# An attention and mixture-of-experts block: all tokens through sorted slots of 256 places, with places, splits and norm roots on GpSimd

## The chip, the cores and the metric

The kernel runs on one core of one Trainium2 chip. The metric is the device time of one execution in microseconds (us). The engines are called PE (TensorE: matmuls and transposes), DVE (VectorE), ACT (ScalarE), POOL (GpSimd) and SP (SyncE, which here only issues DMAs). Each engine works through its own queue in order: an instruction that waits holds up all that stand behind it on the same engine.

## The reference

x has 2 batches of 1024 tokens of 128 numbers, in f32. LN is a layer norm without weights.

```
x = x + LN(attention(LN(x)))     # 8 heads, 2 groups of keys, latent of 32, causal softmax
x = x + LN(moe(LN(x)))

scores = sigmoid(h @ gate.T)                  # 32 experts in 4 groups of 8
keep the 2 groups whose two best (score + bias) add up highest
of their experts keep the 6 with the highest score + bias
w = scores of these 6, divided by their sum, times 0.2
out = sum of w_e * down_e(silu(gate_e h) * up_e h)        # expert width 64
    + shared expert (width 64)
    + 0.1 * the one anchor expert (of 16, width 32) that the best expert points to
```

A token needs the weights of 2 of the 4 groups alone. A group holds 8 experts and 4 anchors: 640 columns, 5 chunks of 128.

## The kernel before, in words

**Schedule.** The order of the instructions on every engine is written out by hand. The main program emits the work of attention and then of the experts. All else is written as Python generators in three lists, `ends`, `moves` and `side`. `tick()` (L251) advances one waking generator in each list by one piece; a `yield n` lets it sleep for n ticks. So each piece's place in the engines' queues is set by the tick at which it is emitted.

**Attention.** There are 16 units (batch, group of keys, block of 256 tokens) and 40 steps in the loop of `attention()` (L590). A step makes the scores `s` (L519) with a bias matmul that subtracts the maxima (L533), the exp on ACT (L539), a mask on POOL on the diagonal (affine_select, L542), the values `o` (L556) and the sums (L565). The maxima come from an earlier pass over the scores (`sm`, L454, L464, reduced on DVE to `nm`, L471). `nm` is split into three bf16 parts on DVE (L487, L489: three casts, two subtractions per unit), which PE transposes (`pm`, L498) into `mT`.

**Routing.** The tokens are four parts of 512. `route` (L669) is a generator per part: output projection `po` (L685), layer norm, sum with x, second layer norm, router logits `pl`, and the choice of groups and experts on DVE. A layer norm's root is `Norm.root` (L335, with its lines L338 and L339): Ln and Exp on ACT, then Newton's step on DVE (L341).

**Sorting.** Three parts are sparse. `place_first` (L971) sorts the first two together, `place_second` (L998) the third: rank matmuls on PE, then operations on DVE give each token two places, and rows of 176 numbers (the token and its weights) are moved to DRAM `placed` by indirect DMAs on POOL (L921), 16 and then 8, each behind a memset (L920), one per tick. Places are in slots of 256, and a slot belongs to one group. `numbered` (L931) makes the slots' group numbers on DVE; `numbers_of` (L949) loads them into registers on PE and SP, and so puts a wait for that DVE work into both queues.

**Slots.** `Slots` (L1035) runs 15 slots. Each fetches its group's weights `wbs` (640 KB, L1025) and its rows `got` (L1062), turns the rows on PE (`pt_s`), writes the weights of the experts to DRAM and reads them back as `spreads`, spread over partitions (L1089, L1094). It makes `pgs` and `pus` on PE (`hidden`, L1111), silu on ACT (L1118), two products on DVE (L1119, L1120), the down projection `ys` on PE (L1134) and writes its 256 results with one DMA from ACT's queue (L1141).

**Dense part.** The fourth part goes through all four groups: `experts` (L1231), 20 chunks of 512 tokens (L1264, L1265, L1278). Beside it, the results of the three sparse parts are gathered by 24 indirect DMAs on POOL (`gather`, at L1203), and `finish` and `normed` add the shared expert, normalize and write out (L1210, L1184).

## Time and profile before

| what | us |
|---|---|
| three runs | 506.69, 508.99, 509.77 |
| median of them | 508.99 |
| the profiled execution | 511.09 |
| its span | 509.4 |
| attention, to its last sums matmul | 0 to 274.2 |
| first matmul of slot 0 | 277.5 |
| slots 0 to 14, to the first matmul of the dense part | 277.5 to 419.2 |
| dense part, to the end of its last matmul | 419.2 to 497.1 |
| tail, to the end of the span | 497.1 to 509.4 |
| PE busy, DVE busy | 429.5, 298.4 |
| ACT busy, POOL busy | 221.9, 84.6 |

The span is the time between the first and the last event on the profile's clock; the profiled execution's own time is 1.7 us longer. In a row of the timeline stand the start, the duration, the engine, the line of the kernel, the operation, out<-in with partitions x elements, how many instructions were put together, and in brackets the idle time before with what ended it. In a row of the groups, the numbers behind the first bar are busy time in us and the mean of one instruction in ns; behind the second bar stands the idle time before such instructions. The granted clock is TensorE's, as a share of full speed.

### The profile page before, as it was taken

What the parts mean: (1) busy time and instruction counts of PE and PEld (TensorE: products, weight loads), DVE (VectorE), ACT (ScalarE), POOL (GpSimd) and SP (SyncE); (2) the same over time, 40 slices, a digit from 0 to 9 for tenths busy, and PEclk for the clock granted to TensorE, in tenths of its full rate; (3) what the DMA queues carried; (4) which work ended last, traced back from release to release, by engine and by line L of the source; (5) the groups of instructions that cost most, each with busy time, mean ns of one, the idle gap of its engine ahead of it and who ended that gap; (6) DMA issues with size and microseconds to landing.
All of it is one profiled execution on the core that took longest, in us unless ns stands there. A gap on an engine that the chain in (4) does not pass through costs nothing.

```text
span 509.4 us, 10160 instructions
## 1 busy us (share of the span) xinstructions
PE 429.5 (84%) x3727; PEld 267.1 (52%) x3727; DVE 298.4 (59%) x1046; ACT 221.9 (44%) x464; POOL 84.6 (17%) x160
## 2 busy tenths in 40 slices
PE   8998979999899999959576479599989989945990
PEld 5554544545445555424234368488888974413430
DVE  4479563786967986986204554343775435415882
ACT  3445654566436766326436126345423322122442
POOL 3000000111001201004821005100000005750100
PEclk9999998999989999989759778799999999977996
DMA  7891000000000000001120825666687694614130
GB/s 204 181 280 44 2 1 2 1 2 3 2 1 3 2 1 1 2 22 53 66 72 16 226 80 153 170 208 200 181 240 226 178 266 113 180 44 134 53 93 21
DMA packets 42946, 47.45 MB, mean 93 GB/s; under 512 B 17392, under 2 KB 35936, under 8 KB 42896
## 3 DMA queue, kind: packets, MB, share of 16 engines
q1 hardware_dynamic: 37520, 39.81, 28.3%
q0 software_dynamic: 1920, 3.74, 2.5%
q10 hardware_dynamic: 3456, 3.25, 2.0%
q8 instruction: 30, 0.49, 0.4%
q14 instruction: 20, 0.16, 0.1%
HBM read 38.06 MB, written 11.34 MB: 97 GB/s over the span
## 4 chain that ended last, share of the span: by engine, by line
PE 46%; DVE 26%; DMA 9%; issue 8%; ACT 4%; POOL 4%; SPq 1%; ACTq 0%; POOLq 0%; DVEq 0%
DVE nm L471 9%; PE sm L454 5%; PE s L519 4%; DMA wbs<-wgu 4%; PE o L556 4%; PE pgs L1111 4%; PE ys L1134 4%; PE pus L1111 3%; POOL placed L921 3%; PE pp L407 3%; PE o L565 3%; PE pg L1264 2%; DMA spreads<-cw_slot 2%; PE pu L1265 2%; PE po L685 2%
## 5 line engine op out<-in xcount | busy, mean ns | idle before, releaser
L471 DVE TENSOR_REDUCE nm<-sm 128x1 f32<-128x512 f32 (+2 forms) x192 | 92.7, 548 | 47.6 <-PE sm L464 24.9
L539 ACT ACTIVATE pr<-s 128x512 f32<-128x512 f32 (+1 forms) x160 | 75.6, 558 | 80.5 <-PE s L533 72.2
L519 PE MATMUL s<-qT,kT 32*128 32x256 f32 (+1 forms) x640 | 54.1, 397 | 10.7 <-DVE pos L901 6.3
L1119 DVE TENSOR_TENSOR hids<-hids,pus 128x512 f32<-128x512 f32 x30 | 20.6, 687 | 51.0 <-PE pus L1111 39.9
L519 PEld LDWEIGHTS s<-qT,kT 32*128 32x128 f32 x640 | 35.3, 190 | 28.6 <-issue 16.2
L556 PE MATMUL o<-pr,v 128*32 128x256 f32 (+1 forms) x640 | 43.3, 387 | 7.3 <-issue 5.5
L542 POOL TENSOR_SCALAR_AFFINE_SELECT pr<-pr 128x1024 f32<-128x1024 f32 x16 | 18.1, 1128 | 187.0 <-ACT pr L539 187.0
L454 PE MATMUL sm<-kT,qT 32*128 32x512 f32 (+3 forms) x384 | 45.8, 533 | 1.5 <-DVE nm L471 1.2
L1134 PEld LDWEIGHTS ys<-wd_sb,hids 128*128 128x128 f32 x300 | 42.3, 201 | 5.9 <-DVE hids L1120 1.8
L1134 PE MATMUL ys<-wd_sb,hids 128*128 x300 | 42.9, 285 | 2.2 <-DVE hids L1120 1.4
L1203 POOL DMA_INDIRECT y<-results,place_of x24 | 23.9, 997 | 110.3 <-PE pg L1264 103.3
L565 PE MATMUL o<-pr,ones 128*32 128x256 f32 (+1 forms) x640 | 40.3, 370 | 1.0 <-issue 1.0
L1111 PE MATMUL pgs<-hTp,wbs 128*128 128x256 f32 x120 | 34.6, 414 | 7.4 <-DMA wbs<-wgu 5.1
L1118 ACT ACTIVATE hids<-pgs 128x512 f32<-128x512 f32 x30 | 17.9, 598 | 35.1 <-PE pgs L1111 33.1
L556 PEld LDWEIGHTS o<-pr,v 128*32 128x32 f32 x640 | 17.6, 113 | 29.2 <-issue 19.0
L1111 PE MATMUL pus<-hTp,wbs 128*128 128x256 f32 x120 | 32.9, 399 | 0.0
L1268 ACT ACTIVATE hid<-pg 128x512 f32<-128x512 f32 x20 | 11.8, 597 | 46.8 <-PE pg L1264 26.5
L921 POOL DMA_INDIRECT placed<-rows,place_of x24 | 23.7, 987 | 50.7 <-DVE place_of L911 46.6
L1269 DVE TENSOR_TENSOR hid<-hid,pu 128x512 f32<-128x512 f32 x20 | 13.6, 682 | 29.8 <-ACT hid L1268 9.7
L1278 PE MATMUL oacc<-hid,wd_sb 128*128 128x512 f32 x40 | 21.8, 627 | 9.9 <-DVE hid L1270 9.9
L1120 DVE TENSOR_TENSOR hids<-hids,spreads 128x512 f32<-128x512 f32 (+1 forms) x45 | 27.1, 603 | 3.6 <-DMA spreads<-cw_slot 2.1
L565 PEld LDWEIGHTS o<-pr,ones 128*32 128x32 f32 x640 | 17.5, 110 | 21.8 <-issue 12.6
(270 smaller groups left out, 643.4 us busy)
## 6 DMA issues: line engine op xcount, KB each, us to landing
wbs<-wgu SPq DMA_DIRECT2D x15, 640.0 KB
spreads<-cw_slot SPq DMA_DIRECT2D x30, 256.0 KB
spreadd<-cw_rows SPq DMA_DIRECT2D x16, 256.0 KB
placed<-zero SPq DMA_DIRECT2D x1, 2640.0 KB
got<-placed SPq DMA_DIRECT2D x15, 176.0 KB
wbd<-wgu SPq DMA_DIRECT2D x4, 640.0 KB
spreads<-cw_slot SPq DMA_DIRECT2D x60, 32.0 KB
results<-ys ACTq DMA_DIRECT2D x15, 128.0 KB
```

The costliest lines, as they stand in the source:

```text
L454: nc.tensor.matmul(banks[r][:, at : at + k1 - k0], lhsT=qT[ts(r, L), g, ts(qt, P)], rhs=kT[ts(r, L), g, k0:k1], start=(at == 0), stop=Fals ...
L471: nc.vector.tensor_reduce(nm[:, k0 // BC, j, r : r + 1], banks[r][:, at : at + k1 - k0], AX.X, ALU.max, negate=True,)
L519: nc.tensor.matmul(banks[r][:, at : at + n], lhsT=kT[rows, g, ts(kt, P)], rhs=qT[rows, g, q * QC + lo : q * QC + lo + n], start=(i == 0), ...
L539: nc.scalar.activation(pr[:, r, 0:m], banks[r][:, 0:m], AF.Exp)
L556: nc.tensor.matmul(o[ts(r, L), lo : lo + n], lhsT=qkv[b][2][:, kt, ts(g, L)], rhs=pr[:, r, at : at + n], start=(kt == 0), stop=False, skip ...
L565: nc.tensor.matmul(o[ts(r, L), QC + lo : QC + lo + n], lhsT=ones32, rhs=pr[:, r, at : at + n], start=False, stop=True, skip_group_check=True,)
L921: move = nc.gpsimd.indirect_dma_start(out=placed[:, :], out_offset=bass.IndirectOffsetOnAxis(ap=place_of[:, k, i : i + 1], axis=0), in_=ro ...
L1111: nc.tensor.matmul(p[:, lo : lo + SL], lhsT=wb[:, m, ts(c, P)], rhs=hT, start=(lo == 0), stop=(c == pair[-1]), skip_group_check=True,)
L1120: nc.vector.tensor_tensor(hid[:, 0:n], hid[:, 0:n], sp[:, pair[0] : pair[-1] + 1, :].rearrange("p c t -> p (c t)"), ALU.mult,)
L1134: nc.tensor.matmul(o[:, ts(j, D)], lhsT=hid[:, at : at + P], rhs=w, start=(c == 0 and j == 0), stop=(c == NC - 1), skip_group_check=True,)
L1203: nc.gpsimd.indirect_dma_start(out=y[k][:, t, :], out_offset=None, in_=results[:, :], in_offset=bass.IndirectOffsetOnAxis(ap=place_of[:, k ...
L1278: nc.tensor.matmul(oacc, lhsT=wd_sb[:, c, :], rhs=hid, start=False, stop=(c == NG * NC - 1))
```

## The change

All four parts go through slots. There are 19 of them, and the dense part, its fetches and the gathers are gone.

- **Places.** Each part is placed by itself, in four sets that continue each other: `place(s)` carries the number of slots used, the last open slot of each group (`base`) and how full it is (`taken`). After the rank matmuls and a copy on ACT, 36 dependent operations on POOL give the places. Each part moves its rows by eight indirect DMAs, with two ticks between them.
- **Order of the slots.** `ordered(s)` runs after parts 1, 2 and 3. It sorts the slots so that full ones come first, with 31, 41 and 4 operations on DVE on one partition, and loads the group numbers into registers of PE, SP and POOL and the slots' numbers into SP's. Slots 5 and on wait for the second order and part 2's moves to be emitted, slots 9 and on for the third and part 3's.
- **Results.** The rows carry four more numbers (ROW is 180): where the token's result in each group belongs. A slot reads its row numbers out with a copy on POOL (`to_row`) and scatters its results by token with two indirect DMAs on POOL, instead of one DMA from ACT's queue. `finish(s)` makes the shared expert of its part between the slots. When slot 14 is emitted (the last part: when all are), it reads both results of 512 tokens with one DMA of 512 KB, adds them (POOL for parts 0 to 2, DVE for the last) and normalizes.
- **Splits.** The five operations on `nm` per unit move from DVE to POOL.
- **Roots.** `Norm.root` is eight operations on POOL with `pow`; Ln and Exp on ACT, the Newton operations on DVE and the table loads for them are gone.
- **Sigmoid.** A part that is routed during attention makes it from Exp on ACT and two operations on DVE.
- **Ticks.** From step 8 of attention two side pieces are advanced per tick.

By engine, the instructions go from 204 to 713 on POOL, 1147 to 954 on DVE, 619 to 585 on ACT, 2679 to 2782 on PE and 381 to 424 on SP. On PE, the first load of group numbers stands in step 32 of attention, behind part 1's rank matmuls in step 30; the second at the end of step 39, ahead of the last values and sums and of slot 0, behind part 2's rank matmuls in step 36; the third in slot 5, behind part 3's rank matmuls in slot 4. Slot 0 and 1's rows are turned in step 37. On POOL, the first `to_row` copy stands ahead of part 2's placing, and the roots and sums of `finish(0)` to `finish(2)` stand ahead of the scatters of slots 16 to 18.

The diff, cut to its core:

```diff
-    sparse, dense = [(0, 0, TB), (0, TB, TB), (1, 0, TB)], [(1, TB, TB)]
-    NTS = sum(n for _, _, n in sparse)
+    parts = [(b, t, TB) for b in range(B) for t in range(0, NT, TB)]
+    NTS = TB * len(parts)
     NS = TOPG * NTS * P // SL + NG - 1
+    full_after = [-(-(TOPG * n * TB * P - NG * (SL - 1)) // SL) for n in (2, 3)]
+    ROW = D + E + A + NG
...
         def root(self):
-            tables(EXP_LN)
-            nc.scalar.activation(self.r0, self.var, AF.Ln, bias=eps_t)
-            nc.scalar.activation(self.r0, self.r0, AF.Exp, scale=-0.5)
-        def newton(self):
-            t, r0 = self.t, self.r0
-            nc.vector.tensor_tensor(t, r0, r0, ALU.mult)
-            nc.vector.scalar_tensor_tensor(t, self.var, EPS, t, ALU.add, ALU.mult)
-            nc.vector.tensor_scalar(t, t, -0.5, 1.5, ALU.mult, ALU.add)
-            nc.vector.tensor_tensor(self.rs, r0, t, ALU.mult)
+            eng, v, t, r0 = nc.gpsimd, self.v, self.t, self.r0
+            eng.tensor_scalar(v, self.var, EPS, None, ALU.add)
+            eng.tensor_tensor(r0, v, minus_half.to_broadcast([P, self.n]), ALU.pow)
+            eng.tensor_tensor(t, r0, r0, ALU.mult)
+            eng.tensor_tensor(t, t, v, ALU.mult)
+            eng.tensor_scalar(t, t, -0.5, 1.5, ALU.mult, ALU.add)
+            eng.tensor_tensor(self.rs, r0, t, ALU.mult)
+            eng.tensor_tensor(t, self.mv[:, :, 0], self.rs, ALU.mult)
+            eng.tensor_scalar(self.nb, t, -1.0, None, ALU.mult)
...
         for k in range(3):
             part = parts[:, :, :, k]
-            nc.vector.tensor_copy(part, m0)
+            nc.gpsimd.tensor_copy(part, m0)
             if k < 2:
-                nc.vector.tensor_tensor(m0, m0, part, ALU.subtract)
+                nc.gpsimd.tensor_tensor(m0, m0, part, ALU.subtract)
...
+        eng = nc.gpsimd
+        eng.tensor_scalar(free, taken, -1.0, float(SL), ALU.mult, ALU.add)
+        eng.tensor_tensor(rest, total, free, ALU.subtract)
+        eng.tensor_scalar(more, rest, 0.0, None, ALU.is_gt)
+        eng.tensor_scalar(new, rest, float(SL), None, ALU.is_gt)
+        eng.tensor_tensor(new, new, more, ALU.add)
...
+        eng.tensor_tensor(pos, rank, wide[0], ALU.subtract)
+        eng.tensor_scalar(pos, pos, 0.0, None, ALU.is_ge)
+        eng.tensor_tensor(pos, pos, wide[1], ALU.mult)
...
+        eng.tensor_tensor(taken, taken, new, ALU.subtract)
+        routed.add(("places", s))
+        yield HOP
+        if s:
+            yield from ordered(s)
+
+    def move_rows(s):
+        yield HOP
+        for k in range(TOPG):
+            for t in range(TB):
+                nc.gpsimd.memset(between, 0.0)
+                move = nc.gpsimd.indirect_dma_start(
+                    out=placed[:, :],
+                    out_offset=bass.IndirectOffsetOnAxis(
+                        ap=place_of[:, k, s * TB + t : s * TB + t + 1], axis=0
+                    ),
+                    in_=rows[s][:, t, :], in_offset=None,
+                )
...
+                yield 2
...
+            for i in range(0, NK, 8):
+                nc.vector.max(order[:, i : i + 8], key)
+                if i + 8 < NK:
+                    nc.vector.match_replace(key, order[:, i : i + 8], key, -2000.0)
...
-                nc.scalar.dma_start(
-                    out=results[ts(i, SL), :].rearrange("(p j) d -> p j d", j=JL),
-                    in_=y.rearrange("p (j d) -> p j d", d=D),
-                )
+                for j in range(JL):
+                    nc.gpsimd.memset(between, 0.0)
+                    move = nc.gpsimd.indirect_dma_start(
+                        out=results[:, :],
+                        out_offset=bass.IndirectOffsetOnAxis(ap=self.to_row[i][:, j : j + 1], axis=0),
+                        in_=y[:, ts(j, D)], in_offset=None,
+                    )
...
+        while some.done < (min(NS, TOPG * 3 * TB * P // SL + NG - 1) if s < 3 else NS):
+            yield 0
+        last = s == len(parts) - 1
...
+        eng = nc.vector if last else nc.gpsimd
+        eng.tensor_tensor(y, y, both[:, :, 1, :], ALU.add)
+        eng.tensor_tensor(own, y, own, ALU.add)
...
-    def experts(b, u):
...
+    for s in range(len(parts)):
+        side += [route(s), place(s)]
+        if s == 1:
+            side.append(some.begin())
     attention()
+    side += [finish(s) for s in range(len(parts))]
     some.run()
-    for b, t0, n in dense:
...
```

## The prediction

> **What bounds the kernel now.** I read the busy table first, then the windows (one row per stage), then the chain of work that ended last, then single rows of the timeline for prices.
>
> ```profile
> span 509.4 us, 10160 instructions
> ...
> PE 429.5 (84%) x3727; PEld 267.1 (52%) x3727; DVE 298.4 (59%) x1046; ACT 221.9 (44%) x464; POOL 84.6 (17%) x160
> ```
>
> TensorE (PE) is the busiest engine, GpSimd (POOL) the idlest. But 84% is a mean over stages. The columns of the windows are start:end, length, then busy time of PE, weight loads, DVE, ACT, POOL, the granted clock, the DMA share and GB/s:
>
> ```profile
> 215.00:247.00 32.00, 25.00 (x322) 12.87 (x322) 22.13 (x91) 15.34 (x37) 10.42 (x17) 0.89 0.11 39
> 247.00:262.00 15.00, 6.36 (x39) 2.56 (x38) 1.21 (x3) 2.89 (x7) 9.54 (x17) 0.54 0.25 83
> ...
> 277.50:331.50 54.00, 38.66 (x186) 33.35 (x187) 25.84 (x112) 20.22 (x41) 10.30 (x21) 0.78 0.54 154
> 331.50:410.30 78.80, 73.15 (x454) 66.21 (x452) 43.26 (x129) 30.54 (x67) 0.00 (x0) 1.00 0.72 209
> 410.30:419.20 8.90, 8.88 (x55) 7.89 (x56) 3.60 (x6) 2.32 (x5) 0.00 (x0) 1.00 0.92 249
> 419.20:497.10 77.90, 64.70 (x153) 28.35 (x151) 43.91 (x98) 23.39 (x36) 27.73 (x27) 0.91 0.39 105
> 497.10:509.40 12.30, 0.66 (x4) 0.42 (x4) 2.92 (x16) 2.96 (x5) 1.26 (x1) 0.65 0.07 22
> ```
>
> Row 4 holds slots 4 to 13 (331.5 to 410.3, by the starts of each slot's first pgs matmul): 78.8/10 = 7.88 us a slot with PE 93% busy. This is the steady price of a slot. Row 3 is slots 0 to 3: 54.0 us where steady would be 31.5, so 22.5 lost to spreads, placing and rows that came late. Row 6 is the dense part, 77.9 us for 512 tokens. Row 7 is the tail behind the last dense matmul. Rows 1 and 2 are the end of attention, with two holes:
>
> ```profile
> 227.17 2.09 PE L519 MATMUL s<-qT,kT 32*128 32x256 f32 x16 [6.31 <-DVE pos L901]
> ```
> ```profile
> 258.24 13.38 issue
> ```
>
> The first is PE idle for 6.3 us ahead of a score matmul: the load of the group numbers into PE's registers stands in front of it and waits for the placing on DVE. The second is from the chain: no wait that the profile shows, for 13.4 us, directly behind 14 row moves that POOL issued back to back. In that time PE did 6.36 of 15 us of work at half the clock. I count about 13 us lost there.
>
> **The change, part by part.** The sum is made against the profiled run: 511.09 us, of which 509.4 is span and 1.7 lies around it. That run stands 0.4% above the median of 508.99.
>
> *Dense part out, four slots in.* 2 x 16 x 128/256 + 3 = 19 slots instead of 15. Out go 77.9 us; in come 4 x 7.88 = 31.5, and about 2 us in which the last slot's own end has no next work over it. Against row 6: -44.4.
>
> *Attention's end.* Before, the two holes cost 6.3 + 13 = 19.3. In the changed order the moves come in four runs of eight with two ticks between, so I drop the second hole; the rows for that are six moves at 304 to 312 us with no hole behind them. The first hole returns in a new form. Between part 1's rank matmuls and the load of the first group numbers stand on PE only sm 0.93+0.40, sums 0.86, s 0.94+0.34, o 0.86, pm 0.34, sm 1.14, sums 0.86, pt_h 0.6, s 0.94+0.40, o 0.86, sm 1.14 (rows of the first 45 us), about 10 us. Behind the load wait steps 32 and on. Against that cover runs a chain: rank 0.8 with its copy on ACT, 36 dependent POOL operations on 128x4 to 128x16 (place), 31 operations on DVE (ordered) at 0.21 start to start (the split rows below), and 1.29 for the register load. A small POOL operation is not in the trace as part of a chain. From below: 0.15, two dependent memsets start to start, or 0.24, the 128x32 sum. From above: 0.73, the 128x256 sum, and for pow 1.27, the 128x512 sum. I take 0.30: nearest is the 128x32 row, plus the gap of 0.05 to 0.1 that dependent pairs show. Chain: 0.8 + 36 x 0.30 + 31 x 0.21 + 1.3 = 19.4; less 10 of cover, a stall of 9.4 (6 at 0.2, 24 at 0.73). Net -9.9: attention ends at 264.3, not 274.2.
>
> ```profile
> L201 POOL TENSOR_TENSOR rep<-rep,ident 128x32 f32<-128x32 f32 x2 | 0.5, 241 | 0.0
> ...
> L704 POOL TENSOR_TENSOR x<-x,an 128x256 f32<-128x256 f32 x8 | 5.8, 726 | 26.7 <-ACT an L360 26.6
> ...
> L1194 POOL TENSOR_TENSOR y<-y,x 128x512 f32<-128x512 f32 x4 | 5.1, 1266 | 44.3 <-DVE y L350 44.3
> ...
> L487 DVE CAST parts<-nm 128x8 bf16<-128x8 f32 x48 | 9.0, 187 | 1.9
> ...
> L489 DVE TENSOR_TENSOR nm<-nm,parts 128x8 f32<-128x8 f32 x32 | 5.5, 172 | 1.1
> ```
>
> *Splits to POOL.* The two DVE groups leave: 14.5 us busy over 16 units, five operations of 1.05 us in a chain per unit. On POOL 5 x 0.30 = 1.5, and a unit's mT, which PE waits for, is later by 0.45 plus what stands before it on POOL (a move 1.27, an affine_select 1.13). PE is 94% busy from 45 to 215 us, so DVE's relief is worth little. I take 0, with -10 (all DVE time were on the path) and +24 (16 units late by 1.5) as ends.
>
> *Roots to POOL.* 8 x 0.30 = 2.4 against Ln, Exp and four or five DVE operations, 1.3 us from 5.24 to 6.57 in the first norm. The first two norms stand in front of everything: +1 each at most, beside weight folding; I take +1. The later ones lie beside attention. Four table loads of 1.28 us in the norms go from ACT, which is no bound: 0.
>
> *Second load, before slot 0.* It is the same chain with 41 DVE operations: 0.8 + 10.8 + 8.6 + 1.3 = 21.5, with 10.5 us of PE work between rank and load. On POOL the first to_row copy, which waits for fetched rows, stands before it: +2. So 13, of which 3.3 stood there before too (274.2 to 277.5, slot 0 waiting for its rows). Slot 0 starts at 264.3 + 13 + 1 = 278.3, +0.8.
>
> *Slots 0 to 18.* 19 x 7.88 = 149.7. Above steady I put 26 where before lost 22.5: route part 3, four psh and four sets of py, now between the slots (11 of PE work by their rows), the fourth row fetch behind part 2's moves (3), and the third chain, rank3 to load to moves of eight rows at 1.27 to fetch (12). The results' scatter costs POOL two indirect DMAs per slot, 2 x 1.27 = 2.5 of 7.88, in place of one issue on ACT: 0, while POOL's queue is short.
>
> *Tail.* Copy 0.6, scatter 2.5, landing 2.3 (moves' rows), read of 512 KB 4.2 (the 640 KB weights' row), two DVE sums 1.4, statistics 1.2, root 2.4, apply on ACT 1.65, sum 0.7, out 5.1 (504.3 to 509.4): 22. The roots and sums of parts 0 to 2 on POOL stand before the last scatters: +3.5. 25.5 in all, where row 7 has 12.3: +13.2.
>
> Sum: 509.4 + 0.8 (slot 0's start) + 4 x 7.88 + 3.5 (above steady) - 77.9 + 2 + 13.2 = 482.5; with 1.7 around it 484.2, and on the median's scale (x 508.99/511.09) 482.
>
> **A rule against it.** The change puts chains of elementwise work onto POOL. The trace has the same 128x512 sum on both engines, 1266 ns on POOL and 692 on DVE, a ratio of 1.83; and a DVE operation of 0.16 us took longer beside an affine_select on POOL:
>
> ```profile
> 242.04 1.11 POOL L542 TENSOR_SCALAR_AFFINE_SELECT pr<-pr 128x1024 f32<-128x1024 f32 x1
> ...
> 242.33 0.85 DVE L344 TENSOR_TENSOR t_moe<-r_moe 128x4 f32<-128x4 f32 x1
> ...
> 243.61 0.16 DVE L347 TENSOR_TENSOR rs_moe<-r_moe,t_moe 128x4 f32<-128x4 f32 x1
> ```
>
> The Trainium skill, "GPSIMD Engine Reference", section 4.1, gives elementwise work to VectorE and calls GpSimd about 2 times slower. Held to small operations that would be 2 x 0.21 = 0.42 us each, and the sum near 506, no gain; by the row of 0.24 plus gap it is 482. Per 0.1 us more, three place chains give 10.8, the splits some 6, the tail's root and backlog 3: about 20 us.
>
> **Rivals.**
> (a) POOL's small operations cost 0.43 us or more (0.30 + 27/200 is where the gain is gone; the 128x256 row of 0.73 and the 0.85 us row speak for it, the 0.24 row against). Place: the wait of PE on both register loads and on mT. At 0.5 us: 482 + 40 = 522, slower.
> (b) The chains are cheap, 0.2 us, or better covered: 482 - 20 = 462. Speaking for it: memsets of 0.11, and DVE freed of 14.5 us.
> (c) DMA bounds the slots. They now have the scatters and three 512 KB reads beside their fetches; the one slot at share 0.92 took 8.9 us. If all did: +19 x 1.0, 501. Against it: shares of 0.65 to 0.81 over slots 4 to 13.
> (d) POOL's 70 indirect DMAs (48 before) bring the unnamed hole again, 13 us: 495.
>
> **How the numbers follow.** Forecast 0.45, (b) 0.17, (c) and (d) together 0.13, (a) 0.25. A measurement of this kernel can tell 1% (about 5 us) from no change. Slower by over 1% (above 514) needs 0.46 us per operation: 0.20 of (a)'s chance; the other 0.05 of (a) and 0.05 of (c) end within 1%; the rest, 0.70, is faster. The range is 457 (case (b) with 5 us of DVE relief) to 518 (case (a) at 0.48 us); the forecast's own is 472 to 493.
>
> **What would show it.** Right: first-to-last pgs at 7.9 us a slot outside three places; PE gaps of some 9 and 11 us ahead of score and sum matmuls with releaser DVE at the two loads; POOL place rows of about 0.3 start to start; slot 0 at 278; 25 us behind the last ys matmul. Wrong: place rows at 0.45 and above, mT waits in each unit, slots above 8.5 us, or DVE rows that grow beside POOL's.

## The result, and the profile after

The changed kernel takes 549.24 us (median of 4 runs, 547.42 to 552.82) where the kernel before took 509.38 (4 runs, 506.69 to 510.89) beside it: a ratio of 1.080 with an interval of 1.072 to 1.087. The forecast was 482, its range 457 to 518. It has the wrong sign. Executions that took over 1.5% longer than the shortest of the same kernel are left out where kernels are compared. The profiled execution took 547.85 us, of which 546.1 is span.

The busy table of the kernel after:

```profile
span 546.1 us, 10716 instructions
...
PE 412.7 (76%) x3787; PEld 276.4 (51%) x3787; DVE 272.4 (50%) x880; ACT 201.3 (37%) x438; POOL 214.8 (39%) x636
```

PE has 17 us less work than before and takes 37 us longer for it: the change did remove work and added waits. The windows of the kernel after, by stages, with the columns as in the prediction (row 1 is attention's steady part, rows 2 to 5 are slots, row 6 is the tail):

```profile
45.00:215.00 170.00, 152.46 (x1878) 81.61 (x1876) 104.99 (x343) 83.11 (x182) 57.84 (x178) 0.97 0.04 6
...
303.00:363.00 60.00, 49.20 (x272) 41.12 (x272) 31.08 (x119) 28.09 (x55) 18.77 (x51) 0.94 0.44 129
363.00:420.00 57.00, 38.20 (x206) 33.41 (x205) 18.05 (x31) 12.21 (x27) 26.48 (x73) 0.88 0.47 143
420.00:480.00 60.00, 50.06 (x282) 44.61 (x281) 23.07 (x38) 17.29 (x40) 15.25 (x31) 0.91 0.57 169
480.00:530.00 50.00, 27.11 (x141) 23.73 (x140) 19.29 (x44) 11.54 (x28) 29.93 (x53) 0.83 0.39 118
530.00:546.00 16.00, 0.00 (x0) 0.00 (x0) 3.23 (x11) 1.65 (x4) 2.50 (x8) 0.50 0.17 50
```

Slots 4 to 13 of the kernel before had PE 93% busy at clock 1.00. Here no stretch of the slots reaches that: 82%, 67%, 83% and, in the last slots, 54%. DMA shares of 0.39 to 0.57 and POOL at 25 to 60% say that neither is full. So I looked for orders and waits, not for a new bound.

The forecast's landmarks against the measured ones, on the profile's clock. A step's landmark is its first bias matmul, a slot's its first `pgs` matmul; what is called "step 38" in times is the stretch from step 37's landmark to step 38's:

| stretch | before | forecast | after | after less forecast |
|---|---|---|---|---|
| start to step 31 | 210.2 | 211.2 | 227.2 | +16.0 |
| steps 31 to 39 | 58.6 | 48.7 | 55.1 | +6.4 |
| step 39 to slot 0 | 8.7 | 18.4 | 19.1 | +0.7 |
| slot 0 to slot 18 | | 168.8 | 204.1 | +35.3 |
| slot 18 to the end | | 35.4 | 40.6 | +5.2 |

The last column adds up to +63.6, the whole error (546.1 less 482.5 of span). The largest part lies in the slots, the next in the steady part of attention. From slot 9's start to slot 17's (412.8 to 489.4), eight slots, it is 76.6/8 = 9.6 us a slot, where the forecast had 7.88. Slots 0 to 8 take 111.4 us, 40 above nine such slots, where the forecast had put 26 above for all that interferes; slot 17 takes 16.1.

### The profile page after: what moved, and what is told of

It is laid out like the page before. It is cut to its first block, busy times and chain, and to the rows that moved or that the text cites. A ratio compares the mean times of both kernels' runs of the same rounds, so it can differ in the third digit from the quotient of the medians.

```text
span 546.1 us, 10716 instructions
## 1 busy us (share of the span) xinstructions
PE 412.7 (76%) x3787; PEld 276.4 (51%) x3787; DVE 272.4 (50%) x880; ACT 201.3 (37%) x438; POOL 214.8 (39%) x636
## 4 chain that ended last, share of the span: by engine, by line
PE 33%; DVE 20%; POOL 17%; DMA 10%; issue 8%; ACT 6%; SPq 4%; ACTq 0%; POOLq 0%; DVEq 0%
DVE nm L475 7%; DMA got<-placed 5%; PE sm L458 4%; PE o L569 3%; PE pgs L1132 3%; PE o L560 3%; SPq L1115 3%; PE pus L1132 3%; DMA y<-results 3%; PE pp L411 3%; PE ys L1155 2%; PE s L523 2%; POOL results L1164 2%; DMA results<-ys,to_row 1%; POOL parts L491 1%
## 5 line engine op out<-in xcount | busy, mean ns | idle before, releaser
L1140 DVE TENSOR_TENSOR hids<-hids,pus 128x512 f32<-128x512 f32 x38 | 26.1, 686 | 103.8 <-PE pus L1132 64.0
L1155 PE MATMUL ys<-wd_sb,hids 128*128 x380 | 55.7, 290 | 16.4 <-DVE hids L1141 16.3
L1155 PEld LDWEIGHTS ys<-wd_sb,hids 128*128 128x128 f32 x380 | 55.6, 207 | 21.2 <-issue 8.9
L1164 POOL DMA_INDIRECT results<-ys,to_row x38 | 39.6, 1043 | 65.5 <-ACT ys L1161 49.2
L523 PEld LDWEIGHTS s<-qT,kT 32*128 32x128 f32 x640 | 34.1, 190 | 21.7 <-issue 10.0
L1132 PE MATMUL pus<-hTp,wbs 128*128 128x256 f32 x152 | 45.0, 424 | 0.0
L1132 PE MATMUL pgs<-hTp,wbs 128*128 128x256 f32 x152 | 44.9, 423 | 0.0
L491 POOL CAST parts<-nm 128x8 bf16<-128x8 f32 x48 | 10.9, 228 | 85.5 <-DVE nm L482 61.5
L939 POOL DMA_INDIRECT placed<-rows,place_of x32 | 31.8, 994 | 23.7 <-DMA got<-placed 16.1
L1141 DVE TENSOR_TENSOR hids<-hids,spreads 128x512 f32<-128x512 f32 (+1 forms) x57 | 39.0, 684 | 2.1
L1132 PEld LDWEIGHTS pus<-hTp,wbs 128*128 128x128 f32 x152 | 33.1, 218 | 5.8
L1132 PEld LDWEIGHTS pgs<-hTp,wbs 128*128 128x128 f32 x152 | 28.5, 207 | 4.6 <-issue 1.5
L1089 PE MATMUL pt_s<-ident,got 128*128 128x128 f32 x38 | 8.4, 306 | 29.1 <-DMA got<-placed 29.0
```

The lines of the kernel that those rows point to most:

```text
L523: nc.tensor.matmul(banks[r][:, at : at + n], lhsT=kT[rows, g, ts(kt, P)], rhs=qT[rows, g, q * QC + lo : q * QC + lo + n], start=(i == 0), ...
L939: move = nc.gpsimd.indirect_dma_start(out=placed[:, :], out_offset=bass.IndirectOffsetOnAxis(ap=place_of[:, k, s * TB + t : s * TB + t + 1 ...
L1132: nc.tensor.matmul(p[:, lo : lo + SL], lhsT=wb[:, m, ts(c, P)], rhs=hT, start=(lo == 0), stop=(c == pair[-1]), skip_group_check=True,)
L1140: nc.vector.tensor_tensor(hid[:, 0:n], hid[:, 0:n], up, ALU.mult)
L1141: nc.vector.tensor_tensor(hid[:, 0:n], hid[:, 0:n], sp[:, pair[0] : pair[-1] + 1, :].rearrange("p c t -> p (c t)"), ALU.mult,)
L1155: nc.tensor.matmul(o[:, ts(j, D)], lhsT=hid[:, at : at + P], rhs=w, start=(c == 0 and j == 0), stop=(c == NC - 1), skip_group_check=True,)
```

## The experiments

The runs were made in five groups on several chips, and the time of the kernel before depends on the chip: 480.85 and 482.36 us (medians) and 482.73 (a single run) on three of them, 506 to 509 elsewhere. The changed kernel takes 549.24, 544.03 (the shortest run) and 546.82 in three groups. So ratios are against the kernel before in the same group, and across groups kernels are compared by landmarks (the changed kernel's slot 0 starts at 301.4, 298.5 and 300.0 us in three profiles, its slot 18 at 505.5, 501.6 and 503.2). Differences under 5 us are not read from them, and late in the slots 5 is not enough: slot 14 starts at 423.7 in loads_later and, in the next group, at 432.5 in sums_dve, and up to there the two do the same work.

### First group: one suspect of the slots, of attention and of the end at a time

**rows_first.** In the kernel before, the fetch of a slot's rows (`fetch_rows`) stood at the second of a slot's three places for issues, ahead of the spreads. The change put it behind them, at the third. The experiment puts it back.

```diff
+                    if k == 1:
+                        self.fetch_rows(i + 3)
                     if k == 2:
                         self.fetch_spread(i + 2)
-                        self.fetch_rows(i + 3)
```

> One move on SP's queue, as it stood before the change: a slot's row fetch (got of slot i+3) is issued ahead of the spreads of slot i+2, not behind them. Theory A: the slots are slow (10.3 us from slot 9 to 18, 7.88 before) because got stands behind six spread issues that wait for DVE's last product of an older slot; it lands 2.4 us after its issue, and PE's turn of the rows waits for it. Then the slots come down to 7.9 to 8.5 us outside the places where a chain interferes, PE's waits for got (29 us in all) mostly go, and the time falls by 25 to 40 us, to 510 to 525. Rival B: the results' scatter and the reads load the DMA engines or POOL, and got is late for that; then the pace stays above 9.5 us and the time above 540.

Measured: 527.50 us (526.58 to 533.09), ratio 1.100 (1.091 to 1.109) against 480.85 on its chip; from slot 9's start to slot 17's it is 60.8/8 = 7.6 us a slot, and slot 18 starts at 485.1 instead of 505.5. The same eight slots in the windows, first of the kernel after, then of rows_first:

```profile
412.80:489.40 76.60, 61.95 (x355) 55.27 (x355) 28.97 (x49) 20.92 (x48) 18.91 (x40) 0.93 0.62 187
```

```profile
407.00:467.80 60.80, 56.92 (x354) 51.93 (x353) 28.81 (x49) 20.73 (x48) 19.20 (x40) 1.00 0.74 223
```

The instructions are nearly the same; PE is 94% busy instead of 81% and the clock stays at 1.00. The DMA share grows to 0.74 with no harm, so DMA did not bound these slots. SP's queue in the kernel after shows the order, and PE its end:

```profile
421.33 1.19 SPq L1110 DMA_DIRECT2D spreads<-cw_slot  x2
422.72 1.99 SPq L1115 DMA_DIRECT2D spreads<-cw_slot  x4
425.07 0.33 SPq L1076 DMA_DIRECT2D got<-placed  x1
425.60 0.35 SPq L1027 DMA_DIRECT2D wbs<-wgu  x1
```

```profile
427.52 0.44 PE L1089 MATMUL pt_s<-ident,got 128*128 128x128 f32 x2 [1.75 <-DMA got<-placed]
```

Six issues of spreads, 3.2 us, stand ahead of `got` on a queue that works in order. The chain of the kernel after over one slot (start, us, what) closes the loop:

```profile
414.98 3.54 DMA got<-placed
...
418.56 0.44 PE pt_s L1089 x2
...
421.05 0.70 DVE hids L1140
421.75 0.08 SPq L1110
...
424.40 0.32 SPq L1115
...
425.07 2.40 DMA got<-placed
```

The rows land and PE turns them; ACT writes their weights to DRAM (419.65), and not before that and DVE's product can SP issue that slot's spreads; behind these it issues the next rows. So each slot hangs on the one before, by a loop through one queue, some 10 us long. In rows_first `got` stands ahead of the next slot's spreads by 4.0 us:

```profile
416.77 0.35 SPq L1027 DMA_DIRECT2D wbs<-wgu  x1
417.37 0.35 SPq L1076 DMA_DIRECT2D got<-placed  x1
421.40 1.17 SPq L1110 DMA_DIRECT2D spreads<-cw_slot  x2
```

The wait views agree (us in total, times, longest), of the kernel after and of rows_first:

```profile
PE pt_s L1089 <- DMA got<-placed: 29.0, 10, 7.9
```

```profile
PE pt_s L1089 <- DMA got<-placed: 6.8, 2, 4.4
```

**results_plain.** It writes a slot's 256 results with the one plain DMA on ACT's queue that the kernel before used; it leaves out the scatter by token, so that `finish` adds other rows.

```diff
-                for j in range(JL):
-                    nc.gpsimd.memset(between, 0.0)
-                    move = nc.gpsimd.indirect_dma_start(
-                        out=results[:, :],
...
+                nc.scalar.dma_start(
+                    out=results[ts(i, SL), :].rearrange("(p j) d -> p j d", j=JL),
+                    in_=y.rearrange("p (j d) -> p j d", d=D),
+                )
```

> Leaves out the scatter by token: a slot's results go in one plain DMA from ACT's queue, in the slots' order, as before the change (the final sums then read rows that are not the tokens'). Theory A (SP's order makes the slots slow): the pace of slots 9 to 18 stays at 9.5 to 10.5 us; the time falls by 2 to 10 us, from the end (two scatters and their landing) and from POOL's queue. Rival B (scatter and its descriptors slow the slots): the pace falls to about 8 us and the time by 25 us or more.

Measured: 524.96 us (521.74 to 525.95), ratio 1.093 (1.087 to 1.098). The slots' pace hardly falls (9.7 us each from 9 to 18), as the theory of the queue's order had it, but the time falls by some 24 us where 2 to 10 were expected. By landmarks that is 7 us at slot 9 (405.5), before any result is read, and 13 at slot 18 (492.7); from slot 18 to the end it is 27.3 instead of 40.6 us. Of this last part, 9 us lie behind the last `ys` matmul (12.0 us to the end, 20.9 in the kernel after) and come with what the run leaves out: in the slots' order the last read takes rows of slots 12 to 15 alone, and SP issues it at 503.97, before slot 18 is done (508.06). About 10 us are left in and behind slots 9 to 18, where the other reads are. SP issues the three reads of 512 KB, first in the kernel after, then in results_plain:

```profile
484.55 11.93 SPq L1228 DMA_DIRECT2D y<-results  x3
```

```profile
475.15 1.56 SPq L1223 DMA_DIRECT2D y<-results  x3
```

Three issues that take 1.56 us when nothing holds them take 11.93, since SP waits for scatters into the same DRAM tile, `results` (us in total, times, longest):

```profile
SPq L1228 <- DMA results<-ys,to_row: 11.7, 2, 10.6
```

A scatter waits for the reads in turn (finish_spaced shows it below). So scattering was not free. How much of it is this mutual wait and how much POOL's issues, the run doesn't separate; the 7 us at slot 9 stay open.

**splits_dve.** The five operations on `nm` go back to DVE.

```diff
-            nc.gpsimd.tensor_copy(part, m0)
+            nc.vector.tensor_copy(part, m0)
             if k < 2:
-                nc.gpsimd.tensor_tensor(m0, m0, part, ALU.subtract)
+                nc.vector.tensor_tensor(m0, m0, part, ALU.subtract)
```

> The five split operations of each attention unit go back to DVE; the rest of the change stays. Theory: in steps 9 to 31 PE waits for the transposes of the split maxima because the splits stand in POOL's queue behind roots (pow 1.04 us), places and row moves; about 12 us of such waits, and the clock falls behind them. Then step 31 starts at 212 to 217 us (227 now, 210 before the change), and the time falls by 8 to 15 us. Rival: the steps are later because of work that is now bunched in attention (two side pieces a tick, five more DVE operations in a chain per unit); then step 31 stays above 223 us and the time falls by less than 4 us.

Measured: 536.12 us (533.73 to 538.33), ratio 1.114 (1.108 to 1.120). Step 31 starts at 218.0 (227.2), step 39 at 269.0 (282.3), slot 0 at 286.7 (301.4), slot 9 at 403.4 (412.8): the splits on POOL had cost 13 to 15 us at the end of attention, a third of which is given back in slots 1 to 8 (9.4 us at slot 9, 11 at slot 18). The reason is the queue, not the price of a split. POOL in the kernel after, while a unit's splits wait:

```profile
150.15 1.26 POOL L939 DMA_INDIRECT placed<-rows,place_of  x1 [0.66 <-issue]
151.71 0.97 POOL L939 DMA_INDIRECT placed<-rows,place_of  x1 [0.18 <-issue]
152.68 0.23 POOL L491 CAST parts<-nm 128x8 bf16<-128x8 f32 x1
```

The split starts the moment that the second move ends; PE's `pm` then starts at 154.12, after 4.66 us of idling. From 84 to 228 us, the waits of `pm` for POOL come to 5.6 + 3.1 + 0.8 = 9.5 us; in splits_dve, `pm` waits 2.4 us from 84 to 218 us, for DVE. Step 31 is still 7.8 us later than before the change (210.2), and the splits don't explain that. The ten steps ahead of it take 65.0 us (153.0 to 218.0) where they took 54.2 (156.0 to 210.2); in them PE is busy for 59.31 instead of 52.41 us with as many matmuls, at a granted clock of 0.89 instead of 1.00. What lowers the clock there was not tried.

**reads_late.** It lets `finish` of parts 0 to 2 read when 17 slots are emitted, not 15, to see whether the finishes' place or their being in one heap counts.

```diff
-        while some.done < (min(NS, TOPG * 3 * TB * P // SL + NG - 1) if s < 3 else NS):
+        while some.done < (NS - 2 if s < 3 else NS):
             yield 0
         last = s == len(parts) - 1
-        yield 0 if last else 8
+        yield 0 if last else 1
```

> The three reads of 512 KB for parts 0 to 2 are emitted behind slot 18's fetches, not ahead of them: they wait for 17 slots instead of 15. Theory: the reads block SP's queue for 12 us (484.6 to 496.5) while they wait for scatters, slot 18's spreads come late, and PE waits 8.5 us; that wait goes, slots 17 and 18 take 8 to 10 us each (9.0 and 16.2 now), and the time falls by 5 to 9 us unless the sums of parts 0 to 2 then end last. Rival: the work of the finishes is only pushed behind the last slot and the tail grows by as much: the time stays within 3 us or rises.

Measured: 548.48 us (544.37 to 549.30), ratio 1.138 (1.131 to 1.145), no gain: slot 17 takes 6.5 us and slot 18 starts at 496.9, and what stood ahead of it stands behind it (50.7 us to the end instead of 40.6).

### Second group: do the gains add, and does the time repeat

**after_again** is the changed kernel, **before_again** the one before, unchanged, in another group.

> The changed kernel, unchanged, beside the others on one chip, as the point from which their edits count. Its steps and slots are expected where its first profile has them, and its time at 545 to 552 us.

> The kernel before, unchanged, to have its profile on a second chip. In the runs so far its time was 509 us on one chip and 481 on another, while step and slot times of the changed kernel agree between the two. Theory: the two holes of 13 and 7.5 us with nothing to wait for, behind back-to-back indirect DMAs, are not always there: where it takes 481 us, steps 37 to 39 take 4 to 5 us each (18.0 for step 38 in the first profile) and the dense part is shorter than 77.9 us. Rival: the whole kernel is faster there, by the clock; then all stages shrink by 5%.

Measured: for the changed kernel 544.03 us in the shortest run and 553.64 to 559.13 in three others, against 506.22 a ratio of 1.075 by the shortest; and 502.89 for the single run of the one before. The landmarks repeat, and so does the hole at attention's end in the kernel before: step 38 takes 17.2 us (18.0 in the first profile).

**rows_splits** joins rows_first and splits_dve.

> Two edits that were tried alone go together: the row fetch ahead of the spreads, and the splits on DVE. Theory: they hold different stretches of time (slots from 9 on; steps 9 to 31 and slot 0's start), so the gains add: about 21 and 13 us below the changed kernel, 512 to 518 us. Rival: they feed the same later wait (the third set's places and moves in slots 4 to 8), which takes some of it back: 518 to 528 us.

Measured: 517.58 us (516.73 to 519.30), ratio 1.023 (1.017 to 1.028). Against the shortest run of after_again, beside it, that is 26.5 us less. The two alone gave 21.7 and 13.1, but against the first result, from another group. At slot 18's start, rows_splits is 28.8 us ahead of after_again (472.8 and 501.6), where the two alone were 20.4 and 11.0 ahead of the first profile. Within what landmarks can tell the gains add: they are different waits.

**reads_pool** is rows_splits with the three reads issued from POOL's queue. If the reads hurt because they block SP's queue, this should free it.

```diff
-        nc.sync.dma_start(
+        (nc.sync if last else nc.gpsimd).dma_start(
             out=both.rearrange("p (t c) -> p t c", t=n),
```

> The two edits together, and the three reads of 512 KB for parts 0 to 2 issued from POOL's queue and not from SP's. Theory: on SP the reads wait for scatters and hold slot 18's spreads and weights; with that gone slot 17 takes 8 to 10 us (17.3 in the run with the row fetch first) and the time falls by 5 to 10 us against the two edits alone. Rival: the sums and roots on POOL then stand earlier before the scatters and ACT waits for the roots as before; less than 3 us.

Measured: 525.65 us (520.76 to 526.94), ratio 1.038 (1.032 to 1.043): 8 us worse than rows_splits beside it. That theory fell. PE now waits 13.66 and 8.15 us for DVE's products, and DVE's queue says why:

```profile
469.56 0.87 DVE L348 BATCH_NORM_STATS2 st_out<-shared 128x6 f32<-128x128 f32 x4 [13.09 <-POOL shared L1240]
...
473.19 0.66 DVE L1140 TENSOR_TENSOR hids<-hids,pus 128x512 f32<-128x512 f32 x1
473.88 1.32 DVE L1141 TENSOR_TENSOR hids<-hids,spreads 128x512 f32<-128x512 f32 x1
```

The statistics of a finish stand in DVE's queue ahead of the slots' products and wait 13.09 us for POOL's sums. These stand on POOL behind a scatter that waits 6.29 us for ACT's `ys` and a read that waits 2.06 us for the scatters. The products, and PE behind them, wait with them.

### Third group: space the finishes, postpone the loads, move the roots

**finish_spaced** is reads_pool's issue at once, with the sums 12 ticks behind it and more ticks between statistics, root and apply, so that nothing stands in a queue before its data is there.

```diff
-        yield 0 if last else 8
+        yield 0
...
-        nc.sync.dma_start(
+        (nc.sync if last else nc.gpsimd).dma_start(
...
-        yield 4
+        yield 4 if last else 12
...
-        yield HOP
+        yield HOP if last else 5
...
-        yield HOP
+        yield HOP if last else 6
```

> On top of the two edits (row fetch first, splits on DVE): parts 0 to 2 are finished in stages that stand further apart. The reads go out at once, from POOL's queue, when slot 14 is emitted; the sums follow 12 ticks later, the statistics 5 later, the apply on ACT 6 ticks behind the roots. Theory C: with the reads off SP's queue PE still waited, so it is not the queue of SP but that DVE's statistics wait for POOL's sums and ACT's apply for POOL's roots, with the products and silu of slots 16 to 18 queued behind them in order (two waits of PE of 9.1 and 8.9 us). Then both waits shrink to under 4 us each and the time falls by 8 to 15 us, to 503 to 510 where the two edits take 517.6. Rival D: POOL's own work (sums, roots, scatters: some 20 us in three slots) is the limit there; then the waits only move and the gain is under 4 us.

Measured: 525.82 us (523.39 to 528.07), ratio 1.091 (1.082 to 1.101). The waits moved and did not go: PE has four gaps of 4.56, 4.56, 6.59 and 3.81 us from slot 18's start on, and a scatter on POOL waits for the reads:

```profile
474.65 1.05 POOL L1164 DMA_INDIRECT results<-ys,to_row  x1 [9.95 <-DMA y<-results]
```

**loads_later** is rows_splits with the loads of group numbers into registers emitted 8 and 18 ticks behind the ordering instead of 2, so that more of attention stands ahead of them on PE.

```diff
-        yield HOP
+        yield (8, 18, HOP)[s - 1]
```

> On top of the same two edits: the register loads of the first and second group numbers are emitted 8 and 18 ticks behind the ordering, not 2. Theory: PE's waits ahead of these loads (12.9 and 12.8 us in the changed kernel's profile) are nothing but the places and the order that are not ready when PE comes to them, and nothing on PE needs the numbers so early; step 33 then takes 6 to 9 us (20.6) and slot 0 starts 6 to 10 us behind step 39 (17.5): 15 to 22 us less at slot 0, and 10 to 20 us in all. Rival: the fetches of slot 0 hang on the same chain through SP; then the waits move to slot 0's rows and weights and less than 6 us are gained.

Measured: 506.74 us (506.17 to 511.60), ratio 1.056 (1.047 to 1.066); 19 us less than finish_spaced beside it. Slot 0 starts at 278.1, where rows_splits had 289.8: 11.7 us earlier, under the 15 to 22 expected. It starts 9.7 us behind step 39 (17.5), as expected, but step 33 takes 16.8 us (20.5), not 6 to 9. PE's stalls at the two loads, first in rows_splits, then in loads_later:

```profile
241.60 0.61 PE L728 MATMUL pl<-upT,hT 128*128 128x32 f32 x2 [12.77 <-DVE nm L475]
```

```profile
285.11 1.93 PE L560 MATMUL o<-pr,v 128*32 128x256 f32 x16 [12.45 <-issue]
```

```profile
239.80 2.24 PE L523 MATMUL s<-qT,kT 32*128 32x256 f32 x11 [9.68 <-DVE nm L475]
```

```profile
275.36 1.51 PE L560 MATMUL o<-pr,v 128*32 128x256 f32 x16 [4.75 <-POOL pr L546]
```

The second stall falls by 7.7 us, the first by 3.1 only: there a score waits for `nm`, whose reductions stand on DVE behind the ordering, which waits for POOL's `base`. What was a wait in PE's own queue is now a wait in DVE's.

**spaced_loads** joins finish_spaced and loads_later: 509.06 us (508.38 to 510.95), ratio 1.059 (1.051 to 1.067), no better than loads_later. It is 16.8 us less than finish_spaced beside it, from which only the loads set it apart: this is what the later loads are worth within one group.

> The two edits, the finishes further apart and the register loads later, together. If the stretches are independent, the gains add: 490 to 500 us, faster than the kernel before on the same chip where that takes 506 to 509, slower where it takes 481. If the third set's chain in slots 4 to 8 takes up what the earlier loads save, 500 to 508 us.

**roots_act** is rows_splits with attention's roots back on ACT (Ln, Exp) and DVE (Newton).

```diff
+            if loaded[0] == EXP_LN:
+                nc.scalar.activation(self.r0, self.var, AF.Ln, bias=eps_t)
+                nc.scalar.activation(self.r0, self.r0, AF.Exp, scale=-0.5)
+                return
             eng, v, t, r0 = nc.gpsimd, self.v, self.t, self.r0
```

> On top of the same two edits: the norm roots of attention's time go back to Ln and Exp on ACT and Newton's step on DVE (those between the slots stay on POOL). Theory: POOL's root takes 2.9 us (pow alone 1.04) and stands ahead of the places in POOL's queue and ahead of ACT's apply; 1 to 1.5 us at the start and 2 to 4 us ahead of each register load come back: 3 to 8 us in all. Rival: the roots lie beside other work; within 2 us.

Measured: 511.69 us (509.49 to 515.48), ratio 1.064 (1.054 to 1.075). Its profiled execution took 519.99 us, so no landmark is read from it, and rows_splits was not run beside it. 511.69 lies 6 us under rows_splits' 517.58 on another chip; what of that the roots are worth is not shown.

### Fourth group: what holds the slots' start and the finishes

The first three start from loads_later, which was not run again beside them; the kernel before takes 507.03 there.

**moves_apart** moves part 3's rows to a DRAM tile that no slot reads, and the last finish reads other data: part 3's results are left out, and the slots no longer wait for these moves.

```diff
-                    out=placed[:, :],
+                    out=(elsewhere if s == 3 else placed)[:, :],
```

> On top of the row fetch first, the splits on DVE and the later register loads (506.7 us). Part 3's rows are moved into a DRAM tile of their own that no slot reads, and the last part's final read takes other data: part 3's results are left out; all instructions and their costs stay. Theory E: in slots 4 to 8 (53 us for 4 slots where 30 are steady) SP's row fetches wait 19 us for the landing of part 3's moves, and the moves for the fetches, because both work on one DRAM tile, in order; with the tiles apart, slots 5 to 8 take 8 to 10 us each (12 to 14.6 now) and slot 9 starts 12 to 18 us earlier against slot 4. Rival F: POOL's and PE's own queues (rank behind to_row, places between scatters) hold the slots; then slot 9 comes less than 6 us earlier.

Measured: 501.83 us (497.47 to 504.24), ratio 0.989 (0.980 to 0.998). Slot 7 takes 8.4 us instead of 14.6, slots 4 to 6 still 13.0, 13.9 and 11.4. From slot 4's start to slot 9's it is 53.8 instead of 60.5 us (58.9 in sums_dve, in the same group): 5 to 7 us. That is near rival F's bound of 6 and far under theory E's 12 to 18. The total holds more than the moves: the last read no longer waits for the last slots' scatters, and behind the last `ys` matmul it is 12.7 us instead of 20.6. In loads_later, SP's queue waits for the moves (330 to 390 us), and in moves_apart that wait is gone:

```profile
SPq L1076 <- DMA placed<-rows,place_of: 19.4, 2, 10.0
```

Of SP's 19.4 us some 5 to 7 are on the path. What makes slots 4 to 6 slow is another thing.

**reads_apart** lets the three early reads take a tile that nothing writes; parts 0 to 2 end with other data.

```diff
-            ],
+            ] if last else wgu[s].rearrange("h k c -> h (k c)")[:, 0 : n * TOPG * D].rearrange(
+                "p (t c) -> p t c", t=n
+            ),
```

> On the same base. The three reads of 512 KB for parts 0 to 2 take as many bytes from a DRAM tile that nothing writes at that time, so no read waits for a scatter and no scatter for a read (parts 0 to 2 then end with other data). Theory G: reads and scatters hold each other up, being on one DRAM tile; slot 17 then takes 8 to 10 us (16.3) and the time falls by 6 to 12 us. Rival H: the three reads' own transfer time (12 us at about 130 GB/s beside the weights) and POOL's sums and roots, with DVE and ACT in order behind them, are the limit: less than 4 us.

Measured: 503.79 us (502.08 to 508.56; five other runs to 514.39), ratio 0.995 (0.990 to 1.001). Its profiled execution took 514.39 us, so no landmark is read from it. By total it stands 6.5 us under sums_dve in the same group, but without loads_later beside it the run puts no number on the mutual wait of reads and scatters.

**sums_dve** puts the nine 128x512 sums of parts 0 to 2 on DVE.

```diff
-        eng = nc.vector if last else nc.gpsimd
+        eng = nc.vector
```

> On the same base. The nine sums of 128x512 of parts 0 to 2 go from POOL (1.27 us each) to DVE (0.69). Theory: DVE's statistics and products come earlier by what POOL took longer (some 3 us), and the product that took 4.2 us beside three sums on POOL takes 0.4 again (3.7): 4 to 8 us less. Rival: DVE's queue now waits for the reads itself, and nothing is gained: within 2 us.

Measured: 510.32 us (507.37 to 512.61), ratio 1.005 (1.001 to 1.008); slot 17's start to the end 52.9 instead of 57.6. That is 4.7 us, no more than landmarks differ by between groups, so a gain is likely but not shown.

**best_try** joins rows_first, splits_dve, loads_later, roots_act and sums_dve.

> The row fetch first, the splits on DVE, the register loads later, attention's roots on ACT and DVE, the last sums on DVE: all that helped or should. If the gains add, 495 to 502 us; the kernel before takes 481 to 509 by chip, so faster than it on some chips alone.

Measured: 506.91 us (504.95 to 512.30), ratio 1.002 (0.998 to 1.006): the same as the kernel before on that chip. With five of its own orders mended, the change gains nothing on that chip; where the kernel before takes 482.36 us, loads_later is 24 us slower than it. No version with the right results is faster than the kernel before in any group. Moves_apart comes under it, and leaves out results.

### Fifth group: the hole of the kernel before

The forecast counted 13 us of gain for the hole behind the back-to-back moves. The kernel before is 25 us faster on some chips, so I ran both kernels on one of these.

> The kernel before once more. On two chips of four it took 481 to 482 us, on the others 506 to 509, and only profiles of the longer runs were seen, with the holes of 13 and 7.5 us behind back-to-back indirect DMAs. Theory: where it takes 481, the holes are what is missing (step 38 in 4 to 6 us, not 17 to 18, and the dense part near 66 us); rival: all stages are shorter by 5%. If this chip gives 506 to 509 again, the profile should repeat the first two.

> The changed kernel once more, beside it. Its steps and slots are expected where its first two profiles have them (slot 0 at 298 to 302 us, slot 18 at 500 to 506) whatever the chip: 542 to 556 us.

Measured: 482.19 us and 546.82 us in single runs, so 64.6 us lie between them there. The windows of the kernel before on this chip, 247 to 262 us:

```profile
247.00:262.00 15.00, 11.56 (x176) 6.54 (x172) 4.08 (x35) 11.42 (x23) 12.03 (x25) 0.95 0.21 69
```

It is the stretch of which the prediction shows 6.36 us of PE work at clock 0.54. Step 38 takes 5.3 us instead of 18.0, with the same 14 moves, most of them 1.27 us apart. And the dense part, first to last pgs, takes 57.7 us, not 72.6 (70.1 in before_again). All other stages agree within 2.5 us. Two holes of about 13 and 15 us come with the chip and not with the program: two profiles have them, from where the kernel takes 506 to 509 us, and the one from a chip where it takes 482 doesn't. What stops the engines in them, the profile doesn't show; that stays open.

## Why the prediction was wrong

**"Slots 0 to 18: 19 x 7.88."** This is the step that failed most. It priced the new slots by the old ones' pace and never listed that the fetch of rows was moved past six issues of spreads on SP's queue, although the diff of `Slots` holds it. Put back, slots 9 to 16 take 7.6 us each and slot 18 starts 20 us earlier. The forecast's own sign that it is wrong ("slots above 8.5") is what the profile shows: 9.6. The term "Above steady I put 26" was too small as well: slots 0 to 8 stand 40 us above steady, and still 36 with the rows put back (300.0 to 407.0). And no single term turns the sign: rows_first, at 527.50, is still slower than the kernel before.

**"Splits to POOL. I take 0."** The price was near, 0.23 and 0.21 us an operation (mean 228 and 207 ns by the groups below) where 0.30 was taken, and the value was mis-sized: 13 to 15 us at attention's end, inside the +24 named. The prediction listed what could stand ahead of a split on POOL (a move, a mask), argued that DVE's relief is worth little, and then took 0 for the delay of `mT` without a reason. That delay is what the runs show. (Its price of "some 6" per 0.1 us would also be 16 x 5 x 0.1 = 8.)

**"The results' scatter ... 0" and the tail's "+3.5".** Counting POOL's issues (2.5 of 7.88 us) found room enough. The profile shows a cost of order: reads and scatters of one DRAM tile wait for each other (11.7 us on SP), and the finishes' statistics on DVE and apply on ACT stand ahead of the slots' products and silu. Results_plain bounds the scatter's part at some 10 us in and behind slots 9 to 18, and 7 before them that were not looked into. PE waits 8.51 and 7.81 us for DVE in the last slots of the kernel after. One of these products is also slow by itself:

```profile
515.60 4.16 DVE L1141 TENSOR_TENSOR hids<-hids,spreads 128x256 f32<-128x256 f32 x1
...
523.65 0.42 DVE L1141 TENSOR_TENSOR hids<-hids,spreads 128x256 f32<-128x256 f32 x1
```

Beside the first POOL runs three 128x512 sums; with these on DVE (sums_dve) the product takes 0.42 us again.

```profile
515.77 3.70 POOL L1249 TENSOR_TENSOR shared<-shared,x 128x512 f32<-128x512 f32 x3
```

The tail itself was priced right: from the last `ys` matmul (525.2) to the end it is 21 us, where the terms without the backlog gave 22.

**"Dense part out: -44.4" and "I count about 13 us lost there".** The two terms fit chips with the holes. Where the dense part takes 15 us less and the hole of 13 isn't there, they hold some 28 us that no change can gain. One profile can't tell; that of the same kernel on a faster chip does.

**Attention's end.** The hole behind the moves is gone, as forecast: step 38 takes 4.3 us (18.0). The chain was priced well: 36 operations of placing from 232.38 to 241.37 us are 0.25 us each (0.30 forecast), 31 of ordering take 8.0 us (6.5). But the stall at the first load was 12.85 us, not 9.4, and 12.75 at the second (13):

```profile
249.82 1.89 PE L728 MATMUL pl<-upT,hT 128*128 128x32 f32 x8 [12.85 <-DVE nm L475]
```

The bracket names DVE's latest work; the order's last operation on DVE (L1009) ends at 248.86, 1 us before PE goes on. The chain starts later than its rank matmul, behind the roots (231.33 less 228.25, 3.1 us) and a mask of 1.11 on POOL, none of which the prediction's chain counted. The groups of POOL, with the root's `pow` as the dearest of the small operations:

```profile
L491 POOL CAST parts<-nm 128x8 bf16<-128x8 f32 x48 | 10.9, 228 | 85.5 <-DVE nm L482 61.5 <-DVE nm L475 21.9
...
L493 POOL TENSOR_TENSOR nm<-nm,parts 128x8 f32<-128x8 f32 x32 | 6.6, 207 | 2.7
...
L356 POOL TENSOR_TENSOR r_moe<-v_moe,minus_half 128x4 f32<-128x4 f32 x4 | 4.2, 1042 | 0.3
```

**The rivals.** (a) had the right sign with the wrong mechanism: the operations cost 0.25 us, far under its 0.43. (b)'s cheap chains were true, and didn't matter. (c) is excluded for slots 9 to 16 by rows_first, where a DMA share of 0.74 goes with 7.6 us a slot. (d)'s hole didn't come. The case that decided, an issue moved behind others on a queue, was among none of them.

**Where the expected gain went.** Of the 63.6 us between forecast and profile, about 20 are the rows' order and 11 the splits, both at slot 18 and each by its experiment; together they give 26 to 29. Later loads give 11.7 more at slot 0 and 16.8 by total within one group. What the finishes cost by the mutual wait and by POOL's sums is not sized. Open: the 7.8 us at step 31 that splits_dve leaves; slots 4 to 6 at 11 to 14 us, where waiting moves explain only slot 7; the share of route and placing of part 3, that stand between these slots, was not tried.

**The rule weighed.** The product of 4.16 us agrees with what the Trainium skill says in "GPSIMD Engine Reference", section 1: GpSimd shares its SBUF interfaces with VectorE, with contention for DVE instructions with two SBUF inputs. In reads_pool's lines above, the product with a PSUM operand (L1140) keeps its 0.66 us beside POOL's sums, and the one with two SBUF operands (L1141) takes 1.32, not 0.69. Section 4.1's factor of about 2, which the prediction held to all small operations, is given there for operations with two inputs. At 128x8 the subtraction takes 207 ns on POOL against 172 on DVE, a ratio of 1.2, and the measurement decides; at 128x512 the ratio was 1.83.

## What to carry to other kernels

A price per instruction decides little where queues are in order: for each instruction that a change puts on a queue or moves on it, a DMA's issue too, write down what stands ahead of it there, what that waits for, and who waits behind it. A loop that runs through a queue (rows, weights, spreads, rows) turns one issue in the wrong place into a longer period for every slot. And before a hole that the profile doesn't explain is counted as a gain, profile the same kernel on other chips.

## What the runs showed of the hardware

- The same program has holes of about 13 and 15 us in two profiles, from where it takes 509.38 and 506.22 us, and none in one from a chip where it takes 482.19, with POOL's moves issued 1.27 us apart on all of them.
- A product with two SBUF operands on DVE took 4.16 us beside three 128x512 sums on POOL, against 0.42 alone, 10 times as long, while POOL's sums took 3.70/3 = 1.23 us, no more than the 1.27 of before. It goes the other way too: in sums_dve a 128x4 product on POOL that takes 0.20 us elsewhere took 0.68, begun while a 128x512 sum of 0.69 us ran on DVE:

```profile
473.60 0.69 DVE L1250 TENSOR_TENSOR shared<-shared,x 128x512 f32<-128x512 f32 x1 [0.58 <-ACT shared L370]
```

```profile
473.67 0.68 POOL L358 TENSOR_TENSOR t_out<-t_out,v_out 128x4 f32<-128x4 f32 x1
```

- On POOL, most operations on 128x4 to 128x16 take 0.19 to 0.26 us whatever their size, and 0.25 from start to start in a chain of 36 (after, 232.38 to 241.37); `pow` on 128x4 takes 1.04.
